# An RWKV block with a gated FFN: sigmoids as tanh, the residual behind the mixes, early TensorE work, another product order in the down projections and a single last store

## The chip, the cores and the metric

The kernel runs on one core of a Trainium2 chip. The metric is device time in microseconds (us), lower is better. A core has TensorE (PE in the profile, with PEld for its weight loads), VectorE (DVE), ScalarE (ACT), GpSimd (POOL) and SyncE (SP); the last two only start transfers here, apart from a few constants. All arithmetic is float32.

## The reference

The input is 2048 tokens of 512 channels. `ln` is a layer norm without gain and bias, `LN` one with them, `shift` moves by one token, and `mix(h, m) = h*m + shift(h)*(1-m)`.

```python
x0 = ln(x)
h = LN1(x0)
k, v, r = mix(h, mk) @ Wk.T, mix(h, mv) @ Wv.T, mix(h, mr) @ Wr.T     # 512 x 512 each
wkv = (e1 * 0 + e2 * v) / (e1 * 0 + e2)      # one step of the recurrence; e1, e2 are exponentials of k
x1 = x0 + (sigmoid(r) * wkv) @ Wo.T
h = LN2(x1)
kk = silu(mix(h, ck) @ Wkey.T)               # 2048 wide
x2 = x1 + sigmoid(mix(h, cr) @ Wcr.T) * (kk @ Wval.T)
y = x + x2
z = ln(y)
out = y + (silu(z @ Wgate.T) * (z @ Wup.T)) @ Wdown.T    # 2048 wide
```

## The kernel before

The tokens are cut into four blocks `b` of 512. Each block goes through a time part (norm, three mixes, `k_unit`, `r_unit`, `v_unit`, `out_unit`), a channel part (norm, two mixes, `gate_unit`, four `up_unit`s, `down_unit`) and, after all four blocks, the FFN (`ffn_gate`, `ffn_up`, `ffn_down`).

A product of 512 x 512 by 512 x 512 is a `unit` of seven quarter products in Strassen's manner (Winograd's form): `step1` to `step7`, each with one accumulator bank of PSUM out of eight. The accumulator `z` is carried through `step1`, `step3`, `step5`, `step6` and `step7`, and between them ScalarE copies it out (`snapshot`, line 473); TensorE may add to `z` again only when that copy has ended. `step2` and `step4` use accumulators of their own, `v` and `x`. The last two steps of a unit are `held` and run between the steps of the next unit (`pop_held`), so that copies have a product or two of cover. Where a unit sums over four weights (`down_unit`, `ffn_down`), a step is four times as long, and the held steps of the unit ahead run inside its `step1`. The sums of weights that the form needs are made once, on VectorE (`prepare`), and kept in DRAM. The small products of the first two blocks are plain (`plain_unit`, line 548): four quarters, each a sum of products over the four channel chunks; only the very first, k of block 0, goes over the chunks first.

TensorE, VectorE and ScalarE run in the order in which the program writes the instructions. Work that isn't in a unit (norms, mixes, sums, the residual) consists of generators in a queue, `background`; after every product `tick` lets so many of their steps run as an assumed cost says, `later` puts a step off by some products, and `need` runs the queue until something named is finished. Each engine then works strictly in its written order, and so does the queue of transfers on SP.

Steps that matter here:

- `time_norm(b)`: statistics, reciprocal root, `scaled` (VectorE, L302), then `shifted_norm`: 16 transposes on TensorE (`transposed`, L349), four evacuations on ScalarE with gain and bias (L361). After them, for blocks 1 to 3, `residual(b)`: two small VectorE operations (`shift`) and four ScalarE operations (L589) that write the tile `x1`. For block 0 the residual is queued behind the mixes.
- `mix`: for each of four channel chunks a scaled copy on ScalarE (`shifted`, L399) and a multiply-add on VectorE (L306); it is at first needed by `k_unit`, which `need`s the key `(b, "k")`. Blocks 2 and 3 add four sums on VectorE (`sums_of`).
- `k_unit`: Relu twice (L645), Exp twice (L650, L651), and a multiply on VectorE. `r_unit`: Sigmoid (L662) and a multiply. `gate_unit`: Sigmoid (L723), used in `down_unit`. `up_unit` and `ffn_gate`: Silu (L733, L819).
- ScalarE holds one set of function tables; where the next function isn't in it, the program has a load (`ACT_TABLE_LOAD`) ahead of the operation.
- `ffn_down`: each quarter is added to `resid` and stored by GpSimd in two pieces of 128 KB (L844).

Of the kernel before, what the change touches and what calls it, by code (L numbers as in the profile page):

```python
# [23 lines left out]
WAIT = 5  # L24
STEP = 1.72
SHARE = 0.88
PP0 = -1e38


# [25 lines left out]
def rwkv_ffn_kernel(  # L55
# [212 lines left out]
    nc.vector.memset(warm, 0.0)  # L268
    nc.scalar.activation(warm, warm, AF.Exp)

    onem = const.tile([P, 5, NC], F32, name="onem")

    nfirst = const.tile([P, NC], F32, name="nfirst")
# [79 lines left out]
            spent[0] += 0.4  # L353
            yield

    def shifted_norm(s, h, hT, g, b):
        nc.vector.tensor_copy(hT[:, :, 0:1], carry[s])
        cost(0)

        def evacuate(c, pt):  # L360
            nc.scalar.activation(  # L361
                hT[:, c, 1:], pt, AF.Identity, bias=vcol(b, c), scale=vcol(g, c)
            )

        yield from transposed(h, evacuate)
        yield 1
        nc.vector.tensor_copy(carry[s], hT[:, :, TB : TB + 1])
        cost(0)
# [18 lines left out]
    def op_done():  # L387
        live_ops[0] -= 1

    def mix(key, hT, row, plain=False):  # L390
        m, B = op_tile("mix")
        ops[key] = B

        def dst(c):
            k = c // 2
            return m[:, 2 * k : 2 * k + 2, c % 2, :]

        def shifted(c):
            nc.scalar.activation(  # L399
                dst(c),  # L400
                hT[:, c, 0:TB].rearrange("p (j t) -> p j t", j=2),
                AF.Copy,
                scale=onem[:, row - MK, c : c + 1],
            )

        shifted(0)
        shifted(1)
        yield 1
        for c in range(NC):
            stt(  # L410
                dst(c),
                hT[:, c, 1:].rearrange("p (j t) -> p j t", j=2),
                vcol(row, c),
                dst(c),
                ALU.mult,
                ALU.add,
            )
            if c + 2 < NC:
                shifted(c + 2)
            yield  # L420
        if not plain:
            yield from sums_of(B)
# [12 lines left out]
            held.pop(0)()  # L435
            tick()

    def unit(weights, Bs, sink, by_token, done=None, free=None):


        acc, tmp = {}, {}
        last = len(weights) - 1

        def product(z, a, b, first, between=None):
            if first:
                acc[z] = bank()
            pz = acc[z]
            wt = [weight(n, a) for n in weights]
            for g, wg in enumerate(wt):
                act = Bs[g][b]  # L450
                for m in range(2):
                    for k in range(2):
                        lo = slice(m * P, (m + 1) * P)
                        lhsT = act[:, k, lo] if by_token else wg[:, k, lo]
                        rhs = wg[:, k, :] if by_token else act[:, k, :]
                        mm = nc.tensor.matmul(  # L456
                            pz[:, m, :],
                            lhsT=lhsT,
                            rhs=rhs,
                            start=first and g == 0 and m == 0 and k == 0,  # L460
                            stop=g == last and k == 1,
                            skip_group_check=True,
                        )
                latest[:] = [mm.ins.name]
                due()
                if g < last:
                    tick()
                    if between is not None and g > 0:
                        between()

        def snapshot(name):
            tmp[name] = q_tile(name)
            nc.scalar.copy(tmp[name], acc["z"])  # L473

        def add(z, name):
            tt(tmp[name], acc[z], tmp[name], ALU.add)

        def step1():
            product("z", A11, B11, True, pop_held)
            snapshot("s1")  # L480

        def step2():
            product("v", A12, B21, True)
            add("v", "s1")
            sink(0, 0, tmp["s1"])

        def step3():
            product("z", S2, T2, False)
            snapshot("u2")

        def step4():
            product("x", S4, B22, True)

        def step5():
            product("z", S1, T1, False)
            snapshot("u4")

            def rest():
                add("x", "u4b")
                sink(0, 1, tmp["u4b"])  # L500

            def both():
                tt(tmp["u2"], tmp["u2"], tmp["u4"], ALU.subtract)
                tmp["u4b"] = tmp["u4"]
                rest()

            later(both, 1)

        def step6():
            product("z", S3, T3, False)  # L510
            sink(1, 1, acc["z"])

        def step7():
            product("z", A22, T4, False)
            add("z", "u2")
            sink(1, 0, tmp["u2"])
            if free is not None:
                free()
            if done is not None:
                later(done, 2)  # L520

        for s in (step1, step2, None, step3, step4, None, step5):
            if s is None:
                pop_held()
            else:
                s()
                tick()
        held.extend((step6, step7))
# [70 lines left out]
    def time_norm(b):  # L599
        xb = xin.pop(b)  # L600
        mv = small.tile([P, NT, 2], F32, tag="mv", name="mv")
        yield from moments(xb, mv)


        var = small.tile([P, 2 * NT], F32, tag="var2", name="var2")
        ts(var[:, :NT], mv[:, :, 1], EPS, None, ALU.add)
        ts(var[:, NT:], mv[:, :, 1], 1.0 + EPS, EPS * EPS, ALU.mult, ALU.add)
        two = small.tile([P, 2 * NT], F32, tag="two", name="two")
        yield from rsqrt(var, two, 2 * NT)
        rstd, both = two[:, :NT], two[:, NT:]  # L610
        h = tok_tile("h")
        yield from scaled(xb, h, mv, both)
        hT = htp.tile([P, NC, TB + 1], F32, tag="hT", name="hT_a")
        hTs[b, "a"] = hT
        if b == 0:
            constants()
        else:
            yield 1
        yield from shifted_norm("a", h, hT, LN1G, LN1B)
        if b == 0:  # L620

            tails.append(residual(b, xb, mv, rstd))
        else:
            yield from residual(b, xb, mv, rstd)

    tails = []

    def time_mix(b, name):
        row = {"k": MK, "r": MR, "v": MV}[name]
# [7 lines left out]
    def k_unit(b):  # L637
        q = qs[b] = {}

        def sink(i, j, c):  # L640
            r = q_tile("r")
            for o in range(2):
                n = 2 * i + o

                nc.scalar.activation(  # L645
                    r[:, o, :], c[:, o, :], AF.Relu, bias=nfirst[:, n : n + 1], scale=-1.0
                )
            e = q_tile("e")
            q[i, j] = e
            nc.scalar.activation(e, r, AF.Exp, scale=-1.0)  # L650
            nc.scalar.activation(r, r, AF.Exp)  # L651

            later(lambda: tt(e, e, r, ALU.mult), 2)

        product_of(b, WK, "k", sink, False)

    def r_unit(b):
        q = qs[b]

        def sink(i, j, c):  # L660
            sg = q_tile("sg")
            nc.scalar.activation(sg, c, AF.Sigmoid)  # L662
            later(lambda: tt(q[i, j], q[i, j], sg, ALU.mult), 1)

        product_of(b, WR, "r", sink, False)

# [22 lines left out]
        return t[:, 2 * j : 2 * j + 2, i * HB : (i + 1) * HB]  # L689

    def out_unit(b):
        def sink(i, j, c):
            v = block_view(x1s[b], i, j)
            tt(v, c, v, ALU.add)
# [25 lines left out]
    def gate_unit(b):  # L720
        def sink(i, j, c):
            s = q_tile("sr")
            nc.scalar.activation(s, c, AF.Sigmoid)  # L723
            gates[b, i, j] = s

        product_of(b, WCR, "cr", sink, True)
# [35 lines left out]
    def down_unit(b):  # L762
        def sink(i, j, c):
            s = gates.pop((b, i, j))
            tt(s, c, s, ALU.mult)
            v = block_view(x1s[b], i, j)
            tt(v, v, s, ALU.add)

        def done():
            nc.sync.dma_start(resid[b], x1s.pop(b))  # L770
# [66 lines left out]
        )  # L837

    def ffn_down(b):
        def sink(i, j, c):  # L840
            v = block_view(rs[b], i, j)
            tt(v, c, v, ALU.add)
            for t in range(2 * j, 2 * j + 2):
                nc.gpsimd.dma_start(  # L844
                    out_t[b][:, t, i * HB : (i + 1) * HB], rs[b][:, t, i * HB : (i + 1) * HB]
                )

        unit([WDN + g for g in range(4)], [Lazy((b, "f", g)) for g in range(4)], sink, True)

# [7 lines left out]
    )  # L859
    push("norm0", time_norm(0))  # L860
    need("norm0")
    background.appendleft((None, time_mix(0, "k"), (0, "k")))
    need((0, "k"))
    for n in "rv":
        push_mix(0, n, time_mix(0, n))
    push("x1", tails.pop())
    credit[1] = 0.5
    k_unit(0)
    prepare_all(early, qp, 2)
# [1 line left out]
    push("norm1", time_norm(1))  # L871
    for n in "krv":
        push_mix(1, n, time_mix(1, n))
    r_unit(0)
    v_unit(0)
    k_unit(1)
# [7 lines left out]
    for b in range(NB):  # L884
# [11 lines left out]
        for g in range(4):  # L896
# [4 lines left out]
            if g == 0:  # L901
                if nxt:
                    push_mix(b + 2, "k", time_mix(b + 2, "k"))
                    push_mix(b + 2, "r", time_mix(b + 2, "r"))
                if b + 1 < NB:
                    push(f"normb{b + 1}", channel_norm(b + 1))
# [82 lines left out]
```

## Time and profile before

| | |
|---|---|
| runs before | 1298.82 us median of 3 (1293.69, 1298.82, 1299.48) |
| the profiled execution's own time | 1299.39 us |
| its span, first to last instruction | 1297.6 us |
| PE busy | 1259.1 us, 97% of the span |
| PEld busy | 1101.6 us, 85% |
| DVE busy | 650.0 us, 50% |
| ACT busy | 363.0 us, 28% |
| POOL busy | 126.4 us, 10% |
| table loads on ACT | 21 of 1.283 us |
| mean granted TensorE clock | 0.992 |

The shares are means over the whole span. The profile's matmul rows are halves: each float32 matmul that the program writes appears as two rows. "Idle before" is time in which an engine had nothing to do ahead of an instruction, with the engine and line that ended it; "issue" is time for which the profile shows no releaser. The granted clock is given as a share of full speed.

### The profile page before, as it was taken

Reading aid. Unit: us, or ns where it says so; the run is one execution under the profiler, and the core shown is the slowest. Engines: PE = TensorE matmul, PEld = TensorE weight load, DVE = VectorE, ACT = ScalarE, POOL = GpSimd, SP = SyncE. Lnnn points to the kernel's source line nnn. Section 1 sums busy time; section 2 is a strip of 40 time slices with the busy share of each in tenths; the row PEclk is TensorE's granted clock in tenths of the full one; section 3 lists DMA queues with packets and bytes.
Section 4 is the critical chain, followed back from the end, with each engine's and each line's share of the span. In section 5 each row is a group of like instructions: output and inputs, shape, how many; then the busy total and the mean of one; then the engine's idle time right before and its main releaser. Section 6 shows DMA issues by size and latency. Waiting matters only on the chain.

```text
span 1297.6 us, 16094 instructions
## 1 busy us (share of the span) xinstructions
PE 1259.1 (97%) x5856; PEld 1101.6 (85%) x5856; DVE 650.0 (50%) x1173; ACT 363.0 (28%) x594; POOL 126.4 (10%) x238
## 2 busy tenths in 40 slices
PE   5989999989999989999999999999999999999997
PEld 4878888868888878888888888888888888888886
DVE  4656668457675586643472474125731364223521
ACT  3562362253532433312310222102320122102200
POOL 0312222110111111112100000000000000000000
PEclk9989999999999999999999999999999999999999
DMA  4745778765676867778755755575556655565551
GB/s 146 260 130 188 272 253 261 241 213 173 199 226 207 276 192 226 217 235 319 242 173 154 249 153 144 161 237 157 143 154 212 192 151 142 162 169 161 150 161 56
DMA packets 120861, 251.71 MB, mean 194 GB/s; under 512 B 15312, under 2 KB 15312, under 8 KB 119760
## 3 DMA queue, kind: packets, MB, share of 16 engines
q1 hardware_dynamic: 102240, 192.46, 50.3%
q0 software_dynamic: 17536, 56.64, 12.0%
q10 hardware_dynamic: 1008, 1.59, 0.3%
q8 instruction: 47, 0.77, 0.3%
q14 instruction: 30, 0.25, 0.1%
HBM read 216.03 MB, written 34.60 MB: 193 GB/s over the span
## 4 chain that ended last, share of the span: by engine, by line
PE 92%; DVE 4%; ACT 2%; issue 1%; DMA 0%; ACTq 0%; POOL 0%; POOLq 0%
PE ps L456 82%; PE ps L548 9%; PE ps L349 2%; DVE u L298 1%; DVE mix L306 1%; DVE mix L298 1%; DMA x<-in_x 0%; ACT r L645 0%; DVE e L298 0%; ACT e L650 0%; ACT r L651 0%; ACT s L473 0%; DVE raw L298 0%; ACT L650 0%; ACT sg L662 0%
## 5 line engine op out<-in xcount | busy, mean ns | idle before, releaser
L456 PE MATMUL ps<-zT,w 128*128 128x256 f32 x1792 | 391.0, 379 | 0.0
L456 PEld LDWEIGHTS ps<-zT,w 128*128 128x128 f32 x1792 | 340.0, 190 | 46.0
L456 PE MATMUL ps<-mix,w 128*128 128x256 f32 x1232 | 279.0, 384 | 8.0 <-ACT s L473 5.6
L456 PEld LDWEIGHTS ps<-mix,w 128*128 128x128 f32 x1232 | 235.6, 193 | 45.0 <-ACT s L473 7.4
L456 PE MATMUL ps<-w,s 128*128 128x256 f32 x1024 | 227.6, 379 | 0.7 <-ACT u L473 0.7
L456 PEld LDWEIGHTS ps<-w,s 128*128 128x128 f32 x1024 | 194.4, 190 | 27.4 <-ACT u L473 1.1
L473 ACT COPY u<-ps 128x512 f32<-128x512 f32 x136 | 79.4, 584 | 462.1 <-PE ps L456 461.8
L298 DVE TENSOR_TENSOR u<-ps,u 128x512 f32<-128x512 f32 x136 | 94.0, 691 | 225.5 <-PE ps L456 222.1
L456 PE MATMUL ps<-w,t 128*128 128x256 f32 x816 | 181.4, 379 | 3.3 <-ACT s L473 2.6
L456 PEld LDWEIGHTS ps<-w,t 128*128 128x128 f32 x816 | 154.6, 190 | 25.3 <-ACT s L473 3.3
L298 DVE TENSOR_TENSOR u<-u,u 128x512 f32<-128x512 f32 x68 | 46.8, 688 | 153.7 <-ACT u L473 153.7
L298 DVE TENSOR_TENSOR s<-ps,s 128x512 f32<-128x512 f32 x84 | 57.9, 689 | 84.2 <-PE ps L456 65.6
L548 PE MATMUL ps<-mix,w 128*128 128x256 f32 x384 | 87.4, 391 | 8.7 <-issue 6.4
L548 PEld LDWEIGHTS ps<-mix,w 128*128 128x128 f32 x384 | 75.4, 197 | 20.2 <-issue 6.6
L844 POOL DMA_DIRECT2D out<-resid x32 | 17.2, 542 | 615.1 <-DVE resid L298 612.7
L127 POOL DMA_DIRECT2D sum<-raw x64 | 34.8, 544 | 275.8 <-DVE raw L298 262.7
L473 ACT COPY s<-ps 128x512 f32<-128x512 f32 x68 | 39.2, 576 | 60.3 <-PE ps L456 48.4
L298 DVE TENSOR_TENSOR raw<-raw 128x512 f32<-128x512 f32 x64 | 43.9, 686 | 22.1 <-DMA raw<-in_w 17.1
L456 PE MATMUL ps<-w,mix 128*128 128x256 f32 x224 | 51.7, 380 | 0.0
L456 PEld LDWEIGHTS ps<-w,mix 128*128 128x128 f32 x224 | 42.2, 190 | 6.6 <-DVE mix L306 0.7
L116 POOL DMA_DIRECT2D raw<-in_w x64 | 34.3, 543 | 117.9 <-PE ps L456 112.5
L298 DVE TENSOR_TENSOR t<-s,t 128x512 f32<-128x512 f32 x64 | 44.2, 691 | 2.1
(100 smaller groups left out, 816.7 us busy)
## 6 DMA issues: line engine op xcount, KB each, us to landing
w<-sum SPq DMA_DIRECT2D x368, 256.0 KB, 2.7
w<-in_w SPq DMA_DIRECT2D x304, 256.0 KB, 2.7
raw<-in_w POOLq DMA_DIRECT2D x64, 256.0 KB, 4.8
sum<-raw POOLq DMA_DIRECT2D x64, 256.0 KB, 3.8
q<-in_w POOLq DMA_DIRECT2D x36, 256.0 KB, 5.3
sum<-q POOLq DMA_DIRECT2D x36, 256.0 KB, 3.9
x<-in_x SPq DMA_DIRECT2D x30, 256.0 KB, 5.3
res<-x SPq DMA_DIRECT2D x4, 1024.0 KB, 6.6
```

The costliest lines, as they stand in the source:

```text
L116: paced(nc.gpsimd.dma_start(t, w[n, k]))
L127: nc.gpsimd.dma_start(sums[n][k], o)
L298: nc.vector.tensor_tensor(out, a, b, op)
L306: nc.vector.scalar_tensor_tensor(out, *args)
L349: nc.tensor.transpose(flat[:, t * P : (t + 1) * P], h[:, t, c * P : (c + 1) * P], ident)
L456: mm = nc.tensor.matmul(pz[:, m, :], lhsT=lhsT, rhs=rhs, start=first and g == 0 and m == 0 and k == 0, stop=g == last and k == 1, skip_gro ...
L473: nc.scalar.copy(tmp[name], acc["z"])
L548: mm = nc.tensor.matmul(acc[i, j][:, m, :], lhsT=act[:, k, lo] if by_token else wg[:, k, lo], rhs=wg[:, k, :] if by_token else act[:, k, : ...
L844: nc.gpsimd.dma_start(out_t[b][:, t, i * HB : (i + 1) * HB], rs[b][:, t, i * HB : (i + 1) * HB])
```

## The change

1. Both sigmoids become `Tanh(0.5 x)`, and the rest of `sigmoid(x) = 0.5 + 0.5 tanh(0.5 x)` goes into the multiplies that follow, which become `scalar_tensor_tensor`; the factor of r is put into the multiply of `k_unit`. The built program has 6 table loads, where it had 21.
2. The residual of every block is queued by itself, behind the k mix (blocks 2 and 3), or behind all three mixes (blocks 0 and 1). `out_unit` needs it.
3. 44 transposes of the identity stand ahead of everything else on TensorE.
4. For block 0 the mix of k is written chunk by chunk, right behind each chunk's evacuation.
5. In units with four weights the order of the steps is 1, 4, 3, 2, 5 where it was 1, 2, 3, 4, 5.
6. In the last unit of all, `u2` is added to `resid` ahead of the last product, and one addition stands behind it instead of two. Output quarters go in one transfer of 256 KB; those of the last block go on SP's queue, behind all its loads.

```diff
+WARM = 44
+    pt = ps.tile([P, 2, HB], F32, tag="ps", name="warm")
+    for _ in range(WARM):
+        nc.tensor.transpose(pt[:, 0, 0:P], ident, ident)
...
-    def shifted_norm(s, h, hT, g, b):
+    def shifted_norm(s, h, hT, g, b, then=None):
...
+            if then is not None:
+                then(c)
...
-    def mix(key, hT, row, plain=False):
+    def mix(key, hT, row, plain=False, at_once=False):
...
+        if at_once:
+            return lambda c: (shifted(c), mixed(c))
+        return mix_steps(B, shifted, mixed, plain)
...
         def step7():
+            if final:
+
+                sink(1, 0, tmp["u2"])
+                product("z", A22, T4, False)
+                sink(1, 0, acc["z"], True)
+                return
...
-        for s in (step1, step2, None, step3, step4, None, step5):
+        order = (step1, step2, None, step3, step4, None, step5)
+        if last > 0:
+
+            order = (step1, step4, step3, step2, step5)
+        for s in order:
...
+        tails[b] = residual(b, xb, mv, rstd)
         if b == 0:
             constants()
+            then = mix((0, "k"), hT, MK, True, True)
+            finished.add((0, "k"))
+            yield from shifted_norm("a", h, hT, LN1G, LN1B, then)
         else:
             yield 1
-        yield from shifted_norm("a", h, hT, LN1G, LN1B)
-        if b == 0:
-
-            tails.append(residual(b, xb, mv, rstd))
-        else:
-            yield from residual(b, xb, mv, rstd)
+            yield from shifted_norm("a", h, hT, LN1G, LN1B)
...
+    def push_residual(b):
+        def run():
+            yield from tails.pop(b)
+
+        push(("x1", b), run())
...
-            later(lambda: tt(e, e, r, ALU.mult), 2)
+            later(lambda: stt(e, e, 0.5, r, ALU.mult, ALU.mult), 2)
...
-            nc.scalar.activation(sg, c, AF.Sigmoid)
-            later(lambda: tt(q[i, j], q[i, j], sg, ALU.mult), 1)
+            nc.scalar.activation(sg, c, AF.Tanh, scale=0.5)
+            later(lambda: stt(q[i, j], sg, 1.0, q[i, j], ALU.add, ALU.mult), 1)
...
     def out_unit(b):
+        need(("x1", b))
...
-            nc.scalar.activation(s, c, AF.Sigmoid)
+            nc.scalar.activation(s, c, AF.Tanh, scale=0.5)
...
-            tt(s, c, s, ALU.mult)
+            stt(s, s, 1.0, c, ALU.add, ALU.mult)
             v = block_view(x1s[b], i, j)
-            tt(v, v, s, ALU.add)
+            stt(v, s, 0.5, v, ALU.mult, ALU.add)
...
     def ffn_down(b):
-        def sink(i, j, c):
+        final = b == NB - 1
+
+        def sink(i, j, c, last=False):
             v = block_view(rs[b], i, j)
             tt(v, c, v, ALU.add)
-            for t in range(2 * j, 2 * j + 2):
-                nc.gpsimd.dma_start(
-                    out_t[b][:, t, i * HB : (i + 1) * HB], rs[b][:, t, i * HB : (i + 1) * HB]
-                )
+            if final and (i, j) == (1, 0) and not last:
+                return
+            eng = nc.sync if final else nc.gpsimd
+            eng.dma_start(
+                out_t[b][:, 2 * j : 2 * j + 2, i * HB : (i + 1) * HB],
+                rs[b][:, 2 * j : 2 * j + 2, i * HB : (i + 1) * HB],
+            )
...
-    background.appendleft((None, time_mix(0, "k"), (0, "k")))
-    need((0, "k"))
     for n in "rv":
         push_mix(0, n, time_mix(0, n))
-    push("x1", tails.pop())
+    push_residual(0)
...
     for n in "krv":
         push_mix(1, n, time_mix(1, n))
+    push_residual(1)
...
                     push_mix(b + 2, "k", time_mix(b + 2, "k"))
+                    push_residual(b + 2)
                     push_mix(b + 2, "r", time_mix(b + 2, "r"))
```

More of the change, by code (lines that the diff above doesn't have):

```diff
@@ L404, in shifted, with mixed @@
             )
[L406 to L409, printed above, removed]
+        def mixed(c):
             stt(
@@ L417, in mix, with mix_steps @@
             )
+        if at_once:
+            return lambda c: (shifted(c), mixed(c))
+        return mix_steps(B, shifted, mixed, plain)
+    def mix_steps(B, shifted, mixed, plain):
+        shifted(0)
+        shifted(1)
+        yield 1
+        for c in range(NC):
+            mixed(c)
             if c + 2 < NC:
@@ L436, in pop_held, with unit @@
             tick()
-    def unit(weights, Bs, sink, by_token, done=None, free=None):
+    def unit(weights, Bs, sink, by_token, done=None, free=None, final=False):
         acc, tmp = {}, {}
@@ L614, in time_norm @@
         hTs[b, "a"] = hT
+        tails[b] = residual(b, xb, mv, rstd)
         if b == 0:
             constants()
+            then = mix((0, "k"), hT, MK, True, True)
+            finished.add((0, "k"))
+            yield from shifted_norm("a", h, hT, LN1G, LN1B, then)
         else:
             yield 1
-        yield from shifted_norm("a", h, hT, LN1G, LN1B)
-        if b == 0:
-            tails.append(residual(b, xb, mv, rstd))
-        else:
-            yield from residual(b, xb, mv, rstd)
-    tails = []
+            yield from shifted_norm("a", h, hT, LN1G, LN1B)
+    tails = {}
+    def push_residual(b):
+        def run():
+            yield from tails.pop(b)
+        push(("x1", b), run())
     def time_mix(b, name):
@@ L839, in ffn_down @@
     def ffn_down(b):
-        def sink(i, j, c):
+        final = b == NB - 1
+        def sink(i, j, c, last=False):
             v = block_view(rs[b], i, j)
             tt(v, c, v, ALU.add)
-            for t in range(2 * j, 2 * j + 2):
-                nc.gpsimd.dma_start(
-                    out_t[b][:, t, i * HB : (i + 1) * HB], rs[b][:, t, i * HB : (i + 1) * HB]
-                )
-        unit([WDN + g for g in range(4)], [Lazy((b, "f", g)) for g in range(4)], sink, True)
+            if final and (i, j) == (1, 0) and not last:
[5 more added lines that the diff above has]
+            )
+        unit(
+            [WDN + g for g in range(4)],
+            [Lazy((b, "f", g)) for g in range(4)],
+            sink,
+            True,
+            final=final,
+        )
     early = [WCR] + [WKEY + g for g in range(4)] + [WVAL + g for g in range(4)]
```

## The prediction

> **What bounds the kernel now.** I read the page first: the busy shares and the chain that ended last.
>
> ```profile
> PE 1259.1 (97%) x5856; PEld 1101.6 (85%) x5856; DVE 650.0 (50%) x1173; ACT 363.0 (28%) x594; POOL 126.4 (10%) x238
> ...
> PE 92%; DVE 4%; ACT 2%; issue 1%; DMA 0%; ACTq 0%; POOL 0%; POOLq 0%
> ```
>
> TensorE sets the time. Its products stay the same in number, so 15 table loads less on ScalarE, 28% busy, are worth nothing by themselves. Only places where TensorE stands still, or runs at a low clock, can pay. The timeline of TensorE alone shows where these are: ahead of 18.52 us, at 63.67 to 70.10, at 274 to 287, at 445 to 457, twice 1.28 us (315.67, 484.33), and in the last 21 us. Between 535 and 1276 us there is no gap. Next I read the chain by time over the first two gaps, and the timeline of ScalarE within the second.
>
> ```profile
> 16.97 0.72 ACT mix L399
> ...
> 17.71 0.76 DVE mix L306
> ...
> 18.52 43.39 PE ps L548 x192
> 61.91 1.76 PE ps L349 x16
> 63.67 6.43 issue
> 70.10 10.05 PE ps L548 x36
> ```
>
> ```profile
> 62.38 2.79 ACT L361 ACTIVATE hT_a<-ps,vec 128x512 f32<-128x512 f32 x4 [13.61 <-PE ps L349]
> 65.67 2.93 ACT L589 ACTIVATE x<-x,shift,two 128x512 f32<-128x512 f32 x4 [0.50 <-DVE shift L302]
> 68.51 1.93 ACT L399 ACTIVATE mix<-hT_a,onem 128x512 f32<-128x512 f32 x3
> ```
>
> At 63.67 TensorE waits for the k mix of block 1, and ScalarE does four residuals (L589) ahead of it. The third view is the chain through the gap of block 2 (that of block 3 is alike).
>
> ```profile
> 271.67 1.28 ACT L650
> ...
> 274.29 0.04 DVE e L298
> 274.33 0.57 issue
> 274.90 0.69 DVE raw L298
> 275.59 0.61 DVE u L298
> ...
> 278.45 0.62 ACT mix L399
> ...
> 279.10 1.41 DVE mix L306 x2
> ...
> 285.73 0.63 ACT sg L662
> 286.36 0.48 ACT s L473
> ```
>
> The last view is the granted clock in slices of 1 us.
>
> ```profile
> 15.00:16.00 1.00, 1.00 (x6) 0.85 (x4) 0.00 (x0) 0.93 (x2) 0.00 (x0) 1.00 0.00 0
> ...
> 19.00:20.00 1.00, 1.00 (x5) 0.84 (x5) 1.00 (x3) 1.00 (x2) 0.00 (x0) 0.82 0.00 0
> 20.00:21.00 1.00, 1.00 (x3) 0.77 (x3) 1.00 (x2) 1.00 (x3) 0.00 (x0) 0.50 0.00 0
> ```
>
> The second pair of columns counts TensorE's starts. Transposes start 6 in a us here and 12 in a us at 62 us, so the first ones ran at half pace. The first matmuls ran at full pace (5 starts), then at half until 23 us: the gap of 2.3 us between the last transpose and 18.52 cost the clock one stretch of 3.4 us.
>
> **Start (parts 3 and 4).** Now all evacuations come first, then all k mixes. After the change ScalarE takes evacuation, mix, evacuation, mix. The first evacuation starts at 13.73 and takes 0.78; the mix needs its result: 14.54 to 15.25 (0.71); VectorE's multiply-add takes 0.75, to 16.03. The cold transposes end at 16.26, so k can start at about 16.2 instead of 18.52: -2.3. The later chunks come every 1.4 us (0.78 + 0.71, less the overlap of 0.1), while the products of a chunk take 16 x 0.216 = 3.5: no new wait. The weights of k were issued by 3.83 us and the transfer engines are empty from 14 us on. The 44 transposes lie ahead of the real ones and can start at 1.4 us, when the identity is written; at the cold pace of 0.21 us each (13.22 to 15.83 for 12 steps) they end by 10.8, ahead of 11.94, when the first real one can start: no cost.
>
> **k of block 1 (part 2).** ScalarE's next free start after the evacuations is 65.05. There the first mix takes 0.71, VectorE 0.75, and TensorE starts at 66.57 instead of 70.10: -3.5. The residual (4 starts, 2.93 us, and two VectorE operations of 0.16) goes into ScalarE's idle stretch of 12.6 us ahead of 103.50, the first sigmoid of block 1; if that cover were gone it would cost its 2.9.
>
> **Table loads (part 1).** The chain shows two loads, 2.56 us, ahead of `u` at 275.5 in block 2. But `u` adds from PSUM and needs the held product, whose last row starts at 274.16; at 0.216 pitch and 0.2 of latency, VectorE can start at 274.58. So only 0.92 of the 2.56 comes back. In block 3 one load (442.91) is on the chain, the last row starts at 445.34, VectorE at 445.76 instead of 446.13: -0.37. Everything behind, two mixes, four sums and two additions on VectorE, then `sg` and the copy that TensorE awaits, stays: a gap of some 3 us remains in either block. The loads elsewhere stand in waits for TensorE or VectorE. The multiplies become scalar_tensor_tensor, 0.745 instead of 0.69: 64 x 0.055 = 3.5 us of VectorE; the two in the gaps' chains take 0.1 each, the rest is covered by VectorE's 50% of idle time, and would cost up to 3.5 without it.
>
> On the size of a load the row is 1.283 us, and the next operation starts 0.02 us behind it. The Trainium skill (ScalarE: Activation LUTs, What ACT_TABLE_LOAD costs) adds a drain of 1.38 to each switch of sets; no drain shows here. By its 2.66 the change would free 39.9 us of ScalarE rather than 19.2, and the held product would still be the limit.
>
> **Residual in blocks 2 and 3.** The mixes of k now go first there, with four multiply-adds on VectorE ahead of the addition for `s<-u` at 181.58. By the new order that addition ends some 0.55 later, and the copy behind it ended at 182.68, 0.1 ahead of the product at 182.78 that awaits it: +0.55. In block 3 the same slot gains 0.3 on ScalarE: no cost.
>
> **Product order (part 5).** No step of a four-weight unit waits in the trace, so there is nothing to gain. The sums for step 4 are needed a step (6.9 us) earlier. The last one is stored at 201.96, lands 3.9 later and loads in 2.7, so is there at 208.6; its product starts at about 217.4. Cover 8.8 us: 0.
>
> **End (part 6).** One addition (0.70 + 0.02) goes. GpSimd started its two stores 0.29 behind the last addition and the data was there after 2.4; a transfer of 256 KB on SP lands in 2.7 (loads; no store of this size on SP is in the trace). So -0.55, bounds -1.2 and +0.5.
>
> **Clock.** At half pace the same matmuls cost more: 64 in 16.10 at 70.10 against 13.98 at 86.03 (2.1); 192 in 43.39 at the start against 41.6 (1.8); 32 in 10.03 and in 8.65 against 7.07 (3.0 and 1.6). Sum 8.5. The gap ahead of k closes; that of block 1 shrinks to 2.9 us. A gap of 0.8 cost no clock here, one of 2.3 did, so those left may or may not. I take 0.7, 1.3 and 3.3 for the last two together, 5.3 in all: -3.2, bounds 0 (all as now) and -8.5 (none left). Where the 44 transposes keep the clock up, block 0 has half of the 0.7; they then end near 9 us, and the 3 us of idle time behind them can lose the clock again.
>
> Whether transposes raise the clock at all: in the trace they did, since the first five matmuls behind them ran at full pace. The Trainium skill (TensorE: Matmul & The Clock Gate, Part 4: PE-mode transpose) says that the release of the clock doesn't engage for them. By that rule the 44 are worth nothing, and k would run cold through its first 3.4 us or more: 1.7 instead of 0.7.
>
> **Sum.** -2.3 - 3.5 - 0.92 - 0.37 + 0.1 x 2 + 0.55 - 0.55 - 3.2 = -10.1. The profiled execution took 1299.39 us, 0.57 above the median of the runs. 1299.4 - 10.1 = 1289.3; I say 1289.
>
> **Rivals.** *The loads were the bound.* If 2.56 us come back in both blocks (+3.8 over my 1.3) and the gaps get short enough to keep the clock (3.3 more): 1282. For it: loads stand on the chain. Against: the held product's row. *The helpers can't follow.* VectorE is busy for 16.1 of the 20 us from 120 to 140; if TensorE, 6 us early, only waits there for sums and norms, 2.3 + 3.5 reappear as new gaps: 1295. Against: nothing from 75 to 262 us waits now, and VectorE's waits there are for TensorE. *ScalarE's order turns on the change.* Residuals now stand among the silus and copies of the `up_unit`s; a group of four is 2.93 us, and the tightest copy has 0.1 to spare. In both blocks the groups are split over two places: four stalls of 2.9 with 1.7 of clock each, 18.4 us: 1307, slower. It decides where a copy leaves less than 2.3 (three residuals) of its cover; in the written order the residuals stand behind an earlier copy, with VectorE's additions still to come, which is against it. That the transposes don't do what they are for is within the clock's bounds.
>
> **Numbers.** 0.5% (6.5 us) is about what a measurement of this kernel can tell from no change: 1292.3 and 1305.3. My forecast (1285 to 1292.5) has 0.68, the loads 0.12, the helpers 0.15 (a fifth of it under 1292.3), the slower case 0.05. Faster 0.68 x 0.97 + 0.12 + 0.03 = 0.81, same 0.14, slower 0.05. The range leaves out the slower case and the tails: 1283.5 to 1295.
>
> **What would show it.** Right: k's first matmul near 16.2; the gap behind the second set of transposes near 2.9; gaps of some 3 us left near 270 and 440 with VectorE's sums in their chain; six loads; one addition behind the last matmul. Wrong: a new wait of TensorE between 75 and 262 us beyond 0.6, or a wait for weights inside `down_unit`.

## The result, and the profile after

| | before | after |
|---|---|---|
| median of 7 runs each | 1294.8 us (1292.06 to 1299.8) | 1286.02 us (1282.65 to 1288.64) |
| ratio after / before, 95% interval | | 0.9924 [0.9899, 0.9948] |
| profiled execution: own time, span | 1299.39, 1297.6 us | 1284.93, 1283.2 us |
| its mean granted TensorE clock | 0.992 | 0.997 |

The change is faster by 8.8 us in the medians. The two profiled executions lie further apart, 14.5 us: that of before is one of its long runs, that of after one of the short runs of its kernel. So the profiles tell where time went, and the medians how much it is.

The first view is the page of after: busy shares, and shares of the chain that ended last.

```profile
PE 1260.0 (98%) x5900; PEld 1104.4 (86%) x5900; DVE 650.4 (51%) x1173; ACT 344.4 (27%) x579; POOL 117.7 (9%) x218
...
PE 95%; DVE 3%; ACT 1%; issue 0%; DMA 0%; ACTq 0%
```

PE has the 44 new transposes and otherwise the same products; its share of the chain went from 92% to 95%. POOL and POOLq are gone from the chain. The next view is the chain through the first two gaps of TensorE (start, length, what).

```profile
13.55 0.73 ACT mix L406
...
14.30 0.76 DVE mix L311
...
15.11 41.71 PE ps L573 x192
56.81 1.76 PE ps L354 x16
58.58 2.99 issue
61.57 18.54 PE ps L573 x77
```

The products of block 0 start at 15.11 instead of 18.52, and 192 of them take 41.71 instead of 43.39. The gap behind the second set of transposes is 2.99 instead of 6.43. ScalarE's timeline over it shows why: no residual stands between the evacuations and the mixes.

```profile
57.29 2.78 ACT L366 ACTIVATE hT_a<-ps,vec 128x512 f32<-128x512 f32 x4 [13.65 <-PE ps L354]
59.95 3.79 ACT L406 ACTIVATE mix<-hT_a,onem 128x512 f32<-128x512 f32 x6
```

The chain through the gap of block 2:

```profile
269.12 0.62 ACT mix L406
...
269.76 1.41 DVE mix L311 x2
...
276.40 0.63 ACT sg L693
277.03 0.48 ACT s L488
...
277.55 12.46 PE ps L471 x49
```

No table load is left in it, yet its second half is as before: mixes and sums on VectorE, then `sg`, then the snapshot copy `s` that TensorE waits for. TensorE's wait for it is 3.0 us in both profiles.

At the end, the last product is followed by one addition on VectorE, at 1279.03; the stores go out on SP, and the span ends 3.5 us behind the addition (1279.72 to 1283.2). Before, it ended 4.4 behind (1293.22 to 1297.6).

Taken together, from profile to profile: start -3.41, gap of block 1 -3.44, block 2's chain -0.90, block 3's -0.37, end -1.63 (-0.72 for the addition, -0.9 behind it), a new stall at 173.7 us +0.43, two small ones -0.15 (+0.3 at 461.4, and 0.45 at 534.3 gone, each with the slower row behind it, 0.32 instead of 0.22), same matmuls at a higher clock -5.0 (1.68 at the start, 0.36 in block 1, 1.45 and 1.48 in blocks 2 and 3). The sum is -14.4, against -14.46 measured.

### The profile page after: what moved, and what is told of

It reads as the page before. It is cut to its first block, busy times and chain, and to the rows that moved or that the text cites. A ratio compares the mean times of both kernels' runs of the same rounds, so it can differ in the third digit from the quotient of the medians.

```text
span 1283.2 us, 16131 instructions
## 1 busy us (share of the span) xinstructions
PE 1260.0 (98%) x5900; PEld 1104.4 (86%) x5900; DVE 650.4 (51%) x1173; ACT 344.4 (27%) x579; POOL 117.7 (9%) x218
## 4 chain that ended last, share of the span: by engine, by line
PE 95%; DVE 3%; ACT 1%; issue 0%; DMA 0%; ACTq 0%
PE ps L471 84%; PE ps L573 9%; PE ps L354 2%; DVE mix L311 1%; DVE u L303 1%; DVE mix L303 1%; DMA x<-in_x 0%; ACT s L488 0%; ACT mix L406 0%; DVE h L307 0%; DVE st L317 0%; ACT r L675 0%; DVE resid L303 0%; DVE e L303 0%; ACT e L680 0%
## 5 line engine op out<-in xcount | busy, mean ns | idle before, releaser
L471 PE MATMUL ps<-mix,w 128*128 128x256 f32 x1232 | 275.4, 381 | 7.4 <-ACT s L488 5.7
L471 PEld LDWEIGHTS ps<-mix,w 128*128 128x128 f32 x1232 | 233.7, 191 | 43.2 <-ACT s L488 7.3
L573 PE MATMUL ps<-mix,w 128*128 128x256 f32 x384 | 85.4, 385 | 4.1 <-issue 3.0
L573 PEld LDWEIGHTS ps<-mix,w 128*128 128x128 f32 x384 | 73.9, 193 | 14.8 <-issue 3.2
L881 POOL DMA_DIRECT2D out<-resid x12 | 8.6, 715 | 497.6 <-DVE resid L303 487.6
```

The lines of the kernel that those rows point to most:

```text
L471: mm = nc.tensor.matmul(pz[:, m, :], lhsT=lhsT, rhs=rhs, start=first and g == 0 and m == 0 and k == 0, stop=g == last and k == 1, skip_gro ...
L573: mm = nc.tensor.matmul(acc[i, j][:, m, :], lhsT=act[:, k, lo] if by_token else wg[:, k, lo], rhs=wg[:, k, :] if by_token else act[:, k, : ...
L881: eng.dma_start(out_t[b][:, 2 * j : 2 * j + 2, i * HB : (i + 1) * HB], rs[b][:, 2 * j : 2 * j + 2, i * HB : (i + 1) * HB],)
```

## The experiments

All times are medians, each beside runs of the kernel before on the same chip, whose median was 1294.75 to 1295.54. Where a kernel ran once, this is said.

**Without the 44 transposes** (one is left).

```diff
-WARM = 44
+WARM = 1
```

> The changed kernel with 1 transpose of the identity instead of 44; everything else as changed. Theory (the 44 are worth little, because the real transposes and the products behind them raise the clock themselves once no gap lies between them): TensorE is at half pace for one stretch of 3.4 us at most around the first products of k, which cost 0 to 1.7 us; the median is 0 to 1.7 us over that of the changed kernel. Rival (the early clock is the main part of the gain at the start): the first 192 products take 43.4 us as in the kernel before instead of 41.7, and the median is 1.7 to 3 us higher. Second rival: no difference at all, the clock is at full pace by the first product anyway.

Measured: 1286.49 us (1284.07 to 1287.73), ratio 0.9925 [0.9902, 0.9949], against 0.9924 for the whole change. The transposes are worth nothing that can be seen in the medians. They do raise the clock: in the windows of after (columns: busy us and starts of PE, PEld, DVE, ACT, POOL; then granted clock, share of the transfer engines, GB/s), the identity's transposes start 7 times in a us until 7 us and 11 times behind it. (The clock column stands at 1.00 in both lines, so this early the starts have to be counted.)

```profile
6.00:7.00 1.00, 1.00 (x7) 1.00 (x6) 0.93 (x5) 0.00 (x0) 0.00 (x0) 1.00 1.04 399
...
8.00:9.00 1.00, 1.00 (x11) 1.00 (x10) 0.83 (x7) 0.00 (x0) 0.00 (x0) 1.00 1.03 391
```

But without them the real transposes, 4.40 us instead of 3.01, leave TensorE no gap ahead of k, whose first row starts at 14.83 instead of 15.11 (x came 0.4 earlier). The clock is full from 16.87 on. Until then k runs at half pace, and the 192 products take 42.70 instead of 41.71: 1.0 us, within the theory's 0 to 1.7, and too little for the medians to show.

**Transposes alone**, on the kernel before (one run).

```diff
+WARM = 44
...
+    pt = ps.tile([P, 2, HB], F32, tag="ps", name="warm")
+    for _ in range(WARM):
+        nc.tensor.transpose(pt[:, 0, 0:P], ident, ident)
```

> The kernel before with nothing but the 44 transposes of the identity at first. Theory (they raise the clock, but it is the gap of 2.3 us between the last real transpose and the first product that loses it): the real transposes run at full pace, the first product starts within 0.5 us of 18.5 less what the data come earlier, the gap grows to 3 us or more, and the clock still falls to half for 3.4 us around the first products; the 192 products take 43 us or more. Rival (the early clock by itself is worth 1.7 us): the 192 products take 41.7 us.

Measured: 1291.47 us, 0.12 under the lowest of the seven runs of before beside it; one time tells nothing here. The 192 products took 41.71, which is the rival's number, but not for its reason. The clock rose early, was lost in the 2.38 us of idle time behind the 44, and the real transposes ran at half pace again:

```profile
10.00:12.00 2.00, 1.05 (x4) 0.48 (x5) 2.00 (x7) 0.00 (x0) 0.00 (x0) 0.98 1.06 408
12.00:14.00 2.00, 2.00 (x10) 2.00 (x11) 0.11 (x2) 1.48 (x2) 0.00 (x0) 0.50 0.48 184
14.00:16.00 2.00, 0.97 (x5) 0.57 (x3) 0.17 (x1) 1.85 (x4) 0.00 (x0) 0.66 0.00 0
```

The granted clock is 0.50 from 12 to 14. The gap of 2.27 us ahead of k at 17.24, as long as the one that cost the clock in the profile of before, did not cost it here: the clock was full from 15.3 on. From the first evacuation to k it is 4.79 us, as in before.

**Sigmoids back**, with the plain multiplies behind them.

```diff
-            later(lambda: stt(e, e, 0.5, r, ALU.mult, ALU.mult), 2)
+            later(lambda: tt(e, e, r, ALU.mult), 2)
...
-            nc.scalar.activation(sg, c, AF.Tanh, scale=0.5)
-            later(lambda: stt(q[i, j], sg, 1.0, q[i, j], ALU.add, ALU.mult), 1)
+            nc.scalar.activation(sg, c, AF.Sigmoid)
+            later(lambda: tt(q[i, j], q[i, j], sg, ALU.mult), 1)
...
-            nc.scalar.activation(s, c, AF.Tanh, scale=0.5)
+            nc.scalar.activation(s, c, AF.Sigmoid)
...
```

> The changed kernel with both sigmoids and their plain multiplies back, so with the table loads of the kernel before. Theory (only what stands in front of the held product's addition counts): TensorE's gap ahead of the third product of v starts and ends 0.9 us later in block 2 and 0.4 later in block 3, measured from the end of the down projection ahead of it; the median is 1 to 3 us higher, with the clock. Rival (each load on the chain counts in full): 2.6 us later in each of the two blocks, and the median is 5 us or more higher.

Measured: 1286.35 us (1284.62 to 1289.85), ratio 0.9928 [0.9904, 0.9952]. The start is the same to 0.01 us in this profile, so its marks can be set beside those of after: the product awaited in block 2 starts at 278.45 instead of 277.55 (+0.90). From there to the one awaited in block 3 it is 167.17 us, against 168.22 in after, of which 1.41 went to a lower clock in after (32 rows in 8.58 instead of 7.17): +0.36. So loads and multiplies together cost 1.3 us in two gaps, as worked out for the loads alone. The median moved by 0.3 only, under the 1 to 3 expected; the runs spread over 5 us, so it can neither show nor deny 1.3.

**Residual back in the norm.**

```diff
             yield from shifted_norm("a", h, hT, LN1G, LN1B)
+            yield from tails.pop(b)
+            finished.add(("x1", b))
...
-    push_residual(1)
...
-                    push_residual(b + 2)
```

> The changed kernel with the residual of blocks 1 to 3 back in the norm, ahead of the mixes. Theory: TensorE's gap ahead of k of block 1 is 6.4 us instead of 3.0, the stall of 0.4 us near 174 us goes, and the median is 3 to 5.5 us higher. Rival (VectorE or ScalarE catches up over the following blocks and the time is lost again there in either kernel): the gap is 6.4 us, but the median is within 1.5 us.

Measured: 1288.19 us (1287.32 to 1291.26), ratio 0.9941 [0.9919, 0.9963]: 2.2 us of the change are gone in the medians, less than the 3 to 5.5 expected, and the two intervals overlap; the profile tells more. ScalarE's timeline has the residual (L614) in its old place:

```profile
57.30 2.78 ACT L366 ACTIVATE hT_a<-ps,vec 128x512 f32<-128x512 f32 x4 [13.65 <-PE ps L354]
60.59 2.93 ACT L614 ACTIVATE x<-x,shift,two 128x512 f32<-128x512 f32 x4 [0.51 <-DVE shift L307]
```

The gap ahead of k of block 1 is 6.42 again, by the chain:

```profile
58.59 6.42 issue
```

The stall at 174 us is gone. Both sides of this part are shown: 3.4 gained in block 1, 0.4 lost in block 2. The last matmul ends 3.1 later than in after.

**Old product order.**

```diff
-        if last > 0:
-            order = (step1, step4, step3, step2, step5)
```

> The changed kernel with the old order of steps (1, 2, 3, 4, 5) in the units with four weights. Theory: nothing waits there in either order; TensorE has no gap inside the down projections, the gaps elsewhere are those of the changed kernel, and the median is within 1.5 us of its 1286. Rival: the order removes the gap of 0.45 us near 535 us, or another one of the channel part, and the old one brings it back: 0.4 to 1 us higher at that place in the profile.

Measured: 1285.98 us (1283.05 to 1288.44), ratio 0.9916 [0.9885, 0.9947]: no difference. No product of `down_unit` or `ffn_down` waits in either. The old order brings a wait of 0.45 us at 522 back (behind a Silu and a copy) and takes one of 0.3 at 461 away, both counted with the slower row behind them.

**Stores as before**, on GpSimd in pieces of 128 KB, those of the other blocks too (one run).

```diff
-            eng = nc.sync if final else nc.gpsimd
-            eng.dma_start(
-                out_t[b][:, 2 * j : 2 * j + 2, i * HB : (i + 1) * HB],
-                rs[b][:, 2 * j : 2 * j + 2, i * HB : (i + 1) * HB],
-            )
+            for t in range(2 * j, 2 * j + 2):
+                nc.gpsimd.dma_start(
+                    out_t[b][:, t, i * HB : (i + 1) * HB], rs[b][:, t, i * HB : (i + 1) * HB]
+                )
```

> The changed kernel with the output stored by GpSimd in pieces of 128 KB as in the kernel before, the single last addition kept. Read from the end of the last addition to the end of the span: 3.5 us in the changed kernel, 4.4 in the one before. Theory (GpSimd's queue has to be emptied at the end of the program, which takes longer than waiting for SP's transfers): 4.3 to 4.5 us again. Rival (the store itself is as fast on either, and the 0.9 us came from something else): 3.5 us.

Measured: 1288.11 us. One time tells nothing at this size; the end of the chain does.

```profile
1281.22 0.70 DVE resid L303
1281.93 0.28 issue
1282.21 0.54 POOL out L881
1282.75 0.53 POOLq L1028
```

From the last addition's end (1281.92) to the end of the span (1286.3) it is 4.4 us, as before, where after has 3.5. GpSimd starts its first store 0.29 behind the addition and spends 0.54 and 0.53 on the two; in after SP issues the one store 0.03 behind it (at 1279.75) and spends 0.37. From the end of the last issue to the end of the span it is 3.0 to 3.1 us in before, in after and here. So the difference lies in the start and the issuing, 0.26 + 0.70, and no longer emptying of GpSimd's queue, which the theory named, shows. The run changes the queue and the size of the pieces together; in after GpSimd spends 0.72 on one store of 256 KB (mean of 12), so by an estimate half of the 0.70 is the second piece and half the queue.

**The copy ahead of `sg`.** The rest of the gaps in blocks 2 and 3 is a question of ScalarE's order. In `step5` the sums that feed `sg` are put off by one product, so that `sg` stands ahead of the snapshot copy in ScalarE's order, and the copy, ready long before, waits with `sg` for VectorE. Putting them off by two products writes the copy first.

```diff
-            later(both, 1)
+            later(both, 2)
```

> The changed kernel with the additions that follow the fifth step of a unit put off by two products instead of one; so ScalarE takes the copy of the next unit's first step ahead of the function that waits for VectorE's sums. Theory (TensorE's gaps of 3.0 and 2.4 us in blocks 2 and 3 and the two of 1.3 us are the copy standing behind that function in ScalarE's order): these four gaps fall below 0.5 us each, and the median is 7 to 11 us lower, the clock included. Rival (VectorE's sums are the bound, the copy only hides it): the gaps move one or two products on with two thirds of their length, and the median is within 3 us. Second rival: later additions hold accumulators longer and new waits arise elsewhere; slower.

Measured: 1276.98 us (1276.31 to 1278.69), ratio 0.9854 [0.9828, 0.988], 9 us under the whole change. ScalarE's timeline:

```profile
271.06 0.58 ACT L488 COPY s<-ps 128x512 f32<-128x512 f32 x1
271.54 1.34 ACT L406 ACTIVATE mix<-hT_b,onem 128x512 f32<-128x512 f32 x2
276.74 0.63 ACT L693 ACTIVATE sg<-u 128x512 f32<-128x512 f32 x1 [3.87 <-DVE u L303]
```

The copy ends at 271.64, not at 277.51; `sg` waits alone, and nobody for it. The gaps of 3.03 and 2.43 and the stall at 174 are gone. The two gaps of 1.28, which come from the same pattern in the channel part (`sr`, then the copy), stayed, against the expectation. There `out_unit` follows, whose operand is itself made by a step put off, so by the program's text it first runs all steps put off (`flush`), and the 2 changes nothing; no run tested this.

**The same edit alone, on the kernel before**, where the sigmoids and their loads are in place.

> The kernel before with nothing but the later additions (copy first). Theory (the copy that stood behind the function was the bound of the gaps in blocks 2 and 3, and the table loads only one part of the way to it): the gaps at 283 and 454 us close as they do in the changed kernel, 7 to 10 us in the median, and the loads on the chain, 2.6 us in either block, are then hidden or cost under 1 us each. Rival (with the loads, the copy is late again): gaps of 1.5 to 3 us remain there, and the gain is under 5 us.

Measured: 1287.29 us (1285.33 to 1289.01), ratio 0.9932 [0.9912, 0.9952]. One number in the kernel before gives 7.6 us, nearly as much as the whole change. ScalarE's timeline in block 2:

```profile
280.16 0.58 ACT L473 COPY s<-ps 128x512 f32<-128x512 f32 x1
280.64 1.34 ACT L399 ACTIVATE mix<-hT_b,onem 128x512 f32<-128x512 f32 x2
281.99 1.28 ACT L662 ACT_TABLE_LOAD   x1
285.84 0.63 ACT L662 ACTIVATE sg<-u 128x512 f32<-128x512 f32 x1 [2.57 <-DVE u L298]
```

The copy ends 5.1 us ahead of `sg`. The gaps of 3.03 and 2.43 close although the table loads still stand there: what bounded them was the order of copy and `sg`.

**Both gaps**: the edit above, and the k mix of block 1 written chunk by chunk like that of block 0, with its products over the chunks first.

```diff
-            later(both, 1)
+            later(both, 2)
...
-            plain_unit(n, B, sink, by_token, done, free, b == 0 and name == "k")
+            plain_unit(n, B, sink, by_token, done, free, name == "k")
...
+        elif b == 1:
+            yield 1
+            then = mix((1, "k"), hT, MK, True, True)
+            yield from shifted_norm("a", h, hT, LN1G, LN1B, then)
+            finished.add((1, "k"))
...
-    for n in "krv":
+    for n in "rv":
```

> The kernel with the later additions (copy first), and in it the k mix of block 1 made chunk by chunk behind each evacuation, as the change has it for block 0, with k of block 1 going over the chunks first. Theory: the gap ahead of k of block 1 shrinks from 3.1 us to about 1.2 (one evacuation 0.78, one mix 0.71, one multiply-add 0.75, less the transposes that run meanwhile), short enough that the clock stays up; median 2 to 3.5 us under the 1277.0 of the kernel with the copy first. Rival: four accumulators end together and out of block 0 waits for ScalarE's eight operations of k; a new gap of 1 to 2 us there takes the gain back, median within 1 us.

Measured: 1273.96 us (1273.48 to 1274.22), ratio 0.9823 [0.9802, 0.9843], the fastest version here. The chain over the gap of block 1:

```profile
57.10 1.76 PE ps L354 x16
58.86 1.13 issue
59.99 12.11 PE ps L573 x55
```

The gap is 1.13 us and the clock stays full from 7.3 to 1270 us. With that, the four runs of this kernel lie within 0.7 us of each other, and the five of the next one within 1.4, where those of after spread over 6 and those of before over 8.

**Both gaps, without the 44 transposes.**

> The fastest kernel so far (copy first, and the k mix of block 1 by chunks) with 1 transpose of the identity instead of 44. Theory (the 44 decide nothing: they end 2 to 4 us ahead of the real transposes, and no gap behind those is long enough to lose the clock): median within 1 us of its 1274.0, the clock at half pace for 3.4 us at most, before 20 us. Rival (here, with every other gap short, they are worth the 1.7 us that one stretch at half pace costs): 1275.5 or more.

Measured: 1274.14 us (1273.02 to 1274.42), ratio 0.9827 [0.9804, 0.9851]. In the quiet kernel too, the transposes make no difference.

## Why the prediction was right, point by point

The forecast was 1289, -10.1 from the profiled 1299.39. It held with the range, but in part by luck: a base that was too high and a gain of clock that the medians do not show partly cancelled, and both came from taking one profile as the usual run.

- *The base.* The profiled execution was taken as 0.57 over the median of three runs. Seven runs put the median at 1294.8, 4.6 below it. The runs of before lie in two groups, near 1294 and near 1299, and three runs could not tell which was the middle. In the 29 beside the experiments, those at 1295.5 or less have a mean granted clock of 0.996 or 0.997, those at 1298.4 or more 0.992 or 0.993, as the profile has; 0.004 of 1297 us is 5 us (an estimate), which is what lies between the groups. From 1294.8 the same sum gives 1284.7, 1.3 under the 1286.02 measured.
- *Start, -2.3.* From the first evacuation (12.73) to k it is 2.38 us, the forecast had 2.47, and before took 4.79. It is 2.37 or 2.38 in all nine profiles with part 4 and 4.78 or 4.79 in all three without it, though no run took part 4 alone out. Mechanism and size were right. The further 1.0 in the profile is mostly x arriving 0.86 earlier; this moves with the run: the first real transpose starts between 10.57 and 11.98 in the twelve profiles, in kernels that differ ahead of it by the 44 transposes alone; x comes early and late with them and without them. The forecast let k wait for the end of the cold transposes; in the last kernel above they are cold again, end at 15.22, and k still starts 2.37 behind its first evacuation (12.89 to 15.26).
- *k of block 1, -3.5.* Measured -3.44, and the residual cost nothing in its new place.
- *Table loads, -0.92 and -0.37, +0.1 twice.* Measured -0.90 and -0.37, and 0.90 and 0.36 with the sigmoids back; these hold the multiplies too, so the two 0.1 do not show. The held product's row was the right limit: 15 loads of 1.283 us less gave 1.3 us. No drain showed around a load either: in the kernel before with the copy first, too, the next operation starts 0.01 behind it, so the 2.66 of the Trainium skill (ScalarE: Activation LUTs, What ACT_TABLE_LOAD costs) is not seen on these runs.
- *Residual in block 2, +0.55.* Measured +0.43, in the slot named.
- *Product order, 0.* The median says 0. The reason was incomplete: the new order moves two waits of 0.3 and 0.45 that no step of the working looked at.
- *End, -0.55.* This term was mis-sized: -1.63 measured, outside its bounds of -1.2 and +0.5. It had set a load of 256 KB on SP (2.7) against a store on GpSimd whose data was there after 2.4, and so expected a loss behind the addition. What counts is from the addition to the end of the span, 3.5 against 4.4. There GpSimd starts 0.26 later and spends 1.07 on two issues against SP's 0.37 on one, which is all of the difference; behind the last issue it is 3.0 to 3.1 us either way.
- *Clock, -3.2.* From profile to profile -5.0. Left of the 8.5 are 1.8 in block 1, 1.5 in block 2, 0.1 in block 3 and none at the start, 3.4 where the forecast had 5.3. For the medians it was mis-sized: the other terms, without the earlier x, make about -8.6, so some -0.2 remains for the clock where the forecast had -3.2; the interval of the ratio allows about 4 us to one side and 2 to the other. The mean granted clocks say the same: the median run of after has 0.996, and the runs of before in the lower group have 0.996 or 0.997.
- *The 44 transposes.* The row against the rule that transposes do not release the clock (the Trainium skill, TensorE: Matmul & The Clock Gate, Part 4: PE-mode transpose) was decided for the row: 7, then 11 starts in a us with nothing but transposes on TensorE. The forecast that the idle time behind them could lose the clock again came true where the transposes stood alone, and in three more profiles: with the copy first, with the old product order and with the stores as before. The first 192 products took 41.71, 42.49 and 44.16 in these three and 41.71 in after, all with the 44; without them they took 42.70 and, in the last kernel, 41.71. So up to 2.5 us can still be lost at the start, and the 44 do not keep it from being lost.

Of the rivals, *the loads were the bound* is out by the edit of one number on the kernel before: the gaps close with all loads in place. *The helpers can't follow* and *ScalarE's order turns on the change* are out by the profile after, with 0.43 us of new waiting between 75 and 262 us. What the prediction listed as staying, "`sg` and the copy that TensorE awaits", held 9 us, by the run with the copy first; it saw the row and did not ask why a copy whose data was ready should stand behind `sg`.

## What to carry to other kernels

When a wait of the busy engine ends with a short copy, look at what stands ahead of that copy in its engine's written order and whether the copy needs it: here a 1 in place of a 2 cost 7.6 us, and the far larger change beside it left it in place. Price a removed operation by what is late next (15 loads, 19 us of ScalarE, gave 1.3). And before a profiled time is taken as base, compare its time and its granted clock with those of several runs.

## What was unexpected of the hardware

The clock is lost in stretches of about 3.4 us, and whether a gap costs one depends on more than its length: 2.26 us ahead of k lost it in the profile of before, 2.27 did not with the transposes alone; 3.03 us in block 2 lost it in after (32 rows in 8.58) and not with the sigmoids back (7.17); and no gap of up to 1.3 us did in any profile looked at. A stretch at half pace costs some 1.7 us (64 rows in 15.74 against 13.98), so the same kernel's runs differ by several us as long as such gaps are in it. Within each profile all changes of the clock lie on one grid of 3.41 us; in before they fall at 16.22, 19.63, 23.05, 67.42, 74.25, 285.87, 292.70, 456.54 and 459.95. The twelve profiles divide by the time that TensorE stood idle in a stretch of this grid which held products and ran at full clock. With 2.02 us or more the next stretch was at half clock (14 cases), with 1.89 or less it was not. Of the gap of 3.03 us, 2.5 fell into one stretch in after (273.62 to 277.03), and at most 1.9 with the sigmoids back (276.56 to 279.97). So by these records the place of a gap on the grid decides, and that place moves from run to run; no run varied this alone. Stretches that held only transposes do not divide so: one with 1.5 us idle lost the clock with the stores as before (9.58 to 12.99), and one with 2.0 kept it without the 44 transposes (57.83 to 61.25).
